# A three-layer field-interaction kernel on one core: bias loads moved to another queue, last weights made earlier, and the end of the last block cut finer

## Chip, core and metric

The kernel runs on one core of one Trainium2 chip, all in fp32. The metric is the device time of one execution in microseconds; the time shown for a kernel is the median of its runs. A profile is one further execution, recorded by the hardware profiler. Its span runs from the first to the last recorded instruction, and the program's own time for that execution is a little longer.

## The reference

```python
B, F, E = 1024, 39, 64          # rows of the input, fields, embedding
HID = [64, 64, 64]

def _cin_layer(Xk, X0, W, b):
    O = W.shape[0]
    Wr = W.reshape(O, Xk.shape[1], X0.shape[1])
    return jnp.einsum('bhe,bfe,ohf->boe', Xk, X0, Wr) + b[None, :, None]

X0 = Xk = sparse_embedding       # (1024, 39, 64)
outs = []
for W, b in ((W0, b0), (W1, b1), (W2, b2)):
    Xk = _cin_layer(Xk, X0, W, b)
    outs.append(Xk.sum(axis=-1))
y = jnp.concatenate(outs, axis=-1) @ fc_w.T + fc_b    # (1024, 1)
```

Each layer multiplies every row of the state with every field of the input, for each embedding position, and mixes the products by a weight. The output needs only sums over the embedding, mixed by `fc_w`.

## The kernel before

**The algebra.** There is no function between the layers, so the last two layers fold into a second linear map of the same pair products. Write P for the products x_a * x_b of two fields (a <= b, with a row of ones as a fortieth field), for one batch row and one embedding position. Then X1 = W0 P, and a second set of 64 rows Z = W' P comes from W1, W2 and `fc_w`. The output of a batch row is the sum over the embedding of (X1 + b0) * (Z + fc0), over 64 rows, plus the fields weighted by 39 numbers made of W2, fc2 and b1, plus one constant made of b1, b2 and fc_b. `wfin` holds the final weights: 64 ones, and below them the 39 weights of the fields. `kfin` is the constant. Both are made on the chip by `last_weights`, which multiplies b1 (present twice, in 128 rows, as `b1s`) with a prepared table `v2`.

**Tiling.** The batch is cut into 32 blocks of 32 batch rows, so 2048 columns (batch row x position). The 819 pair products of a block are packed in six chunks of 128 rows (`PAIRS`), and a small chunk of 32 pair rows for two blocks at once. A chunk's product `p` (128x2048) is one VectorE multiply of two gathered tiles of `rt`. The gathers (`roll`, `roll_small`, L172) are indirect DMAs issued from GpSimd (POOL). They read tables `xd` in DRAM, three of them, each for two blocks; `load` (L166) fills a table from the input and `fill_ones` (L362) writes its row of ones.

**Steps.** `steps` lists (block, chunk): for each pair of blocks n, n+1 the six chunks of n, the small chunk (c = 6, done by `join`, L576 and L587, on 32x64 tiles of the array for both blocks), then the six chunks of n+1. A step's `multiply` (L556) adds its product into four banks `po[n][m]`, one for each quarter m of 512 columns. An fp32 matmul call is two weight loads and two matmuls in the trace, so that a step is 8 matmuls of 512 columns. The order of work is written out by hand: the code emits, step by step, PE's `multiply` of a step and VectorE's `product` four steps ahead (`AHEAD`), with four product buffers. When the chunks of a block are done, `finish` makes z = Z + fc0 on ScalarE (L604), g = (X1 + b0) * z on VectorE (L606) and sums g over the embedding into `sums` (L617). `fields` (L599) has put the block's 39 fields below g, so that the same reduction sums them.

**Start.** A prologue builds index lists and the weights of the chunks: `weight_rows` adds the two orders of a pair, `spread` copies the small chunk's rows, and `weight_turn` transposes a chunk's weights on PE into a bank `tr` (four to a bank, kept in `turned`) and copies them to `wa`. The small vectors are loaded from GpSimd after the gathers of block 1: b0 twice, then b1, b2 and fc_b. GpSimd's queue goes on with `fill_ones(2)` and, in the main loop, with the gathers of the next blocks. SP's queue carries `fill_ones(1)` and the loads of blocks 2 and 3 at the end of step 0, and most later loads. At step 11 (`at == NPAIR + 5`) `spread_b1` doubles b1 with a matmul by `twice`, and at step 12 `last_weights` makes `wfin` and `kfin`, in a bank of its own.

**End.** The last `TAIL` = 2 steps go by quarters: for each quarter m both chunks are multiplied and then `finish_quarter` takes that quarter through z, g and the sum, while PE does the next quarter. Then the final product of `wfin` with `sums` comes in three parts: 512 and 504 columns of the output, and the last 8, which need the last quarter. The first two are copied out with `kfin` by ScalarE (L755), the last by VectorE (L757); ACT's queue stores the first 1016 numbers, SP's queue the last 8.

Of the kernel before, what the change touches and what calls it, by code (L numbers as in the profile page):

```python
# [72 lines left out]
NPAIR = len(PAIRS)  # L73
SQUARE = 32
NCHUNK = NPAIR + 2
MM = 512
SUB = 1024
BLK = 2048
# [4 lines left out]
BB = BLK // E  # L83
SB = SUB // E
NBLK = B // BB
NTAB = 3

U_STEPS = ((10, -29), (20, -8), (23, -2), (25, -36), (28, 32))
V_STEPS = ((0, -3), (20, 6), (25, 33), (28, -35), (31, -39))
# [56 lines left out]
def cin_kernel(ctx: ExitStack, tc: tile.TileContext, x, w0t, b0, w1, b1, w2, b2, fc_w, fc_b, out):  # L146
    nc = tc.nc
# [3 lines left out]
    const = ctx.enter_context(tc.tile_pool(name="const", bufs=1))  # L151
# [39 lines left out]
    bias = const.tile([H, 2], F32, name="bias")  # L191
# [3 lines left out]
    fcb = const.tile([1, 1], F32, name="fcb")  # L195
    wfin = const.tile([H + F, 1], F32, name="wfin")
    kfin = const.tile([1, 1], F32, name="kfin")
# [25 lines left out]
    with prep as prep:  # L223
# [20 lines left out]
        nc.vector.memset(fc2, 0.0)  # L244
        nc.vector.memset(v2, 0.0)
        nc.vector.memset(warm, 0.0)
        nc.sync.dma_start(fcrow, fc_w)
        def load_half(k):
            nc.scalar.dma_start(
# [111 lines left out]
        def fill_ones(k, engine, src):  # L361
            engine.dma_start(xd[k][F::FT].rearrange("r (p c) -> p r c", c=128), src)  # L362
# [33 lines left out]
        for k in range(2):  # L396
            for u in range(2):
# [5 lines left out]
                    start=True,  # L403
                    stop=True,
# [22 lines left out]
        column = blocks.rearrange("h k (f j) -> h (k f) j", j=32)[:, :, 0]  # L427
# [27 lines left out]
        for k, n in enumerate((8, 5)):  # L455
            for t in range(2):
                m = (n + 1 - t) // 2
# [9 lines left out]
        nc.vector.tensor_scalar(lists[:, 2 * NT :], both_of, 2.0, seat, ALU.mult, ALU.add)  # L467
        roll_small(0)
        roll(1)
        for h in (0, H):  # L470
            nc.gpsimd.dma_start(b0s[h : h + H], b0.rearrange("(h o) -> h o", o=1))
        for k, t in enumerate((b1, b2)):
            nc.gpsimd.dma_start(bias[:, k : k + 1], t.rearrange("(h o) -> h o", o=1))
        nc.gpsimd.dma_start(fcb, fc_b.rearrange("(p o) -> p o", o=1))
        fill_ones(2, nc.gpsimd, ones)
        w1v = w1s.rearrange("o (h f) -> o h f", f=F)
        groups = [(k, min(NA * k, F - NA)) for k in range(4)]
        for k, a in groups:
# [4 lines left out]
                start=True,  # L483
                stop=True,
# [46 lines left out]
    turned = []  # L531

    def weight_turn(c):
        place = len(turned) % 4 * 128
        if not place:
            tr = bank("tr")
        else:
            tr = turned[-1]
        turned.append(tr)
        nc.tensor.transpose(tr[:, place : place + 128], pairs[:, c], unit)  # L540
        nc.scalar.copy(wa[:, c, 0 : 2 * H], tr[:, place : place + 2 * H])  # L541
        nc.scalar.copy(wa[:, c, 2 * H :], tr[:, place : place + H])

    work = ctx.enter_context(tc.tile_pool(name="work", bufs=2))
    sums = const.tile([H + F, B], F32, name="sums")
    po, g = {}, {}
# [2 lines left out]
        if n not in po:  # L549
            po[n] = [bank("po") for _ in range(BLK // MM)]  # L550

    def multiply(n, c, p, quarters=range(BLK // MM)):
        open_block(n)
        for m in quarters:
            side = m % 2 * H
            nc.tensor.matmul(  # L556
                po[n][m],
                wa[:, c, side : side + 2 * H],
                p[:, bass.ts(m, MM)],
                start=n % 2 == 0 and c == 0,  # L560
                stop=n % 2 == 1 and c == NPAIR - 1,
            )

    def join(n, p):
# [37 lines left out]
    def finish_bank(n, m, z):  # L602
        one, other = slice(m % 2 * H, m % 2 * H + H), slice((m + 1) % 2 * H, (m + 1) % 2 * H + H)
        nc.scalar.activation(z[one], po[n][m][other], AF.Identity, bias=fc0s[other])  # L604
        at = bass.ts(m % 2, MM)
        return lambda: nc.vector.scalar_tensor_tensor(  # L606
            g[n][m // 2][0:H, at], po[n][m][one], b0s[one], z[one], ALU.add, ALU.mult
        )

    def finish(n):  # L610
# [10 lines left out]
                    ALU.add,  # L621
                )

    def finish_quarter(n, m):
        z = work.tile([128, MM], F32, name="z", tag="z")
        finish_bank(n, m, z)()
        b_at = n * BB + m * MM // E
        nc.vector.tensor_reduce(
            sums[:, b_at : b_at + MM // E],
            g[n][m // 2][:, bass.ts(m % 2, MM)].rearrange("p (b e) -> p b e", e=E),  # L630
            AX.X,
            ALU.add,
        )

    def spread_b1(pk):
        nc.tensor.matmul(
            pk[:, 2:3],
            twice[0:H].rearrange("p h s -> p (h s)"),
            bias[:, 0:1],
            start=True,  # L640
            stop=True,
        )
        nc.scalar.copy(b1s, pk[:, 2:3])

    def last_weights(pk):

        for low, at, n in ((1, 0, 32), (0, 32, F - 32)):
            nc.tensor.matmul(
                pk[at : at + n, 0:1], v2v[:, low, 0, 0:n], b1s, start=True, stop=True
            )  # L650
        fc1 = v2v[:, 0, 0, F - 32 : FT - 32]
        nc.tensor.matmul(pk[0:1, 1:2], b1s, fc1, start=True, stop=False)
        nc.tensor.matmul(
            pk[0:1, 1:2], bias[:, 1:2], columns[0:H, 2:3], start=False, stop=True
        )
        nc.vector.memset(wfin[0:H], 1.0)
        nc.scalar.copy(wfin[H : H + F], pk[0:F, 0:1])
        nc.scalar.activation(kfin, pk[0:1, 1:2], AF.Identity, bias=fcb, scale=float(E))

    AHEAD = 4  # L660
    TAIL = 2
    steps = []
    for n in range(0, NBLK, 2):
        steps += [(n, c) for c in range(NPAIR + 1)] + [(n + 1, c) for c in range(NPAIR)]
# [3 lines left out]
    p = {}  # L668
# [18 lines left out]
    n, c = steps[3]  # L687
# [61 lines left out]
    outv = out.rearrange("b o -> o b")  # L749
    done = B - MM // E  # L750
    for lo, hi in ((0, MM), (MM, done), (done, B)):
        py = bank("py")[0:1, 0 : hi - lo]
        nc.tensor.matmul(py, wfin, sums[:, lo:hi], start=True, stop=True)
        if hi < B:
            nc.scalar.activation(y[:, lo:hi], py, AF.Identity, bias=kfin)  # L755
        else:
            nc.vector.tensor_scalar(y[:, lo:hi], py, kfin, None, ALU.add)  # L757
    nc.scalar.dma_start(outv[:, 0:done], y[:, 0:done])
    nc.sync.dma_start(outv[:, done:B], y[:, done:B])


# [40 lines left out]
```

## Time and profile before

| what | value |
|---|---|
| time of the kernel, median of 3 runs | 735.9 us (734.88 to 737.36) |
| the profiled execution | 734.91 us |
| its span | 733.1 us |
| granted TensorE clock | 1.0 |
| ScalarE, GpSimd busy | 167.7 us, 402.0 us |
| gathers r L172 (156, on POOL) | 1932 ns mean |
| b0 columns L471 (2 issues on POOL) | at 39.14, 8.4 us to landing |
| b1 and b2 columns L473 (2 issues on POOL) | at 40.25, 7.9 us to landing |
| loads of blocks 2 and 3 (2 issues on SP, L166) | at 24.12, 1.78 us of issuing |
| first gather of block 2 (POOL) | at 46.09, after 2.49 us idle |
| store of the last 8 outputs (SP, L759) | issued at 731.01 |

PE is TensorE's matmuls, PEld its weight loads, DVE is VectorE, ACT is ScalarE, POOL is GpSimd and SP is SyncE. A q behind a name is that engine's queue of DMA issues. L556 is line 556 of the kernel. All times are microseconds from the span's start unless marked ns. In a row of a timeline, the bracket at the end tells how long the engine was idle before, and which instruction's end released it. This releaser is inferred: a wait for several things is put down to the one that came last in the records.

### The profile page before, as it was taken

Reading aid. Unit: us, or ns where it says so; the run is one execution under the profiler, and the core shown is the slowest. Engines: PE = TensorE matmul, PEld = TensorE weight load, DVE = VectorE, ACT = ScalarE, POOL = GpSimd, SP = SyncE. Lnnn points to the kernel's source line nnn. Section 1 sums busy time; section 2 is a strip of 40 time slices with the busy share of each in tenths; the row PEclk is TensorE's granted clock in tenths of the full one; section 3 lists DMA queues with packets and bytes.
Section 4 is the critical chain, followed back from the end, with each engine's and each line's share of the span. In section 5 each row is a group of like instructions: output and inputs, shape, how many; then the busy total and the mean of one; then the engine's idle time right before and its main releaser. Section 6 shows DMA issues by size and latency. Waiting matters only on the chain.

```text
span 733.1 us, 6351 instructions
## 1 busy us (share of the span) xinstructions
PE 728.0 (99%) x2377; PEld 314.9 (43%) x2377; DVE 638.4 (87%) x520; ACT 167.7 (23%) x241; POOL 402.0 (55%) x254
## 2 busy tenths in 40 slices
PE   9999999999999999999999999999999999999998
PEld 4444444444444444444444444444444444444443
DVE  6979799988889888898988889888898888889885
ACT  3322121222212222121221212221122221212222
POOL 7769998537555455654547545455654447535300
PEclk9999999999999999999999999999999999999999
DMA  8887898979575796757778675896767876566700
GB/s 291 305 318 294 300 355 304 383 293 331 232 270 231 287 355 252 281 226 262 314 287 304 245 275 226 305 353 219 279 246 275 313 286 264 214 253 245 287 0 1
DMA packets 65979, 197.23 MB, mean 269 GB/s; under 512 B 40109, under 2 KB 40174, under 8 KB 45980
## 3 DMA queue, kind: packets, MB, share of 16 engines
q0 software_dynamic: 28784, 185.56, 65.3%
q1 hardware_dynamic: 35464, 9.28, 5.5%
q10 hardware_dynamic: 1700, 1.99, 0.9%
q8 instruction: 18, 0.29, 0.1%
q14 instruction: 13, 0.11, 0.0%
HBM read 196.76 MB, written 10.60 MB: 283 GB/s over the span
## 4 chain that ended last, share of the span: by engine, by line
PE 93%; DVE 2%; POOL 2%; DMA 1%; issue 1%; ACT 0%; DVEq 0%
PE po L556 86%; PE po L576 4%; PE po L587 2%; DMA b0s<-in_b 1%; POOL r L172 1%; DVE p L217 1%; PE idle L276 1%; POOL u L172 1%; DVE g L606 1%; POOL v L172 0%; DVE pairs L523 0%; PE pv L399 0%; PE pt L479 0%; PE pw L411 0%; DVE sums L617 0%
## 5 line engine op out<-in xcount | busy, mean ns | idle before, releaser
L556 PE MATMUL po<-p,wa 128*128 128x512 f32 x1536 | 665.7, 594 | 0.7 <-DVE p L217 0.6
L217 DVE TENSOR_TENSOR p<-r 128x2048 f32<-128x2048 f32 (+2 forms) x197 | 433.8, 2235 | 74.5 <-PE po L556 69.9
L556 PEld LDWEIGHTS po<-p,wa 128*128 128x128 f32 x1536 | 289.7, 190 | 371.3 <-issue 350.5
L172 POOL DMA_INDIRECT r<-xd,lists x156 | 301.4, 1932 | 263.9 <-issue 259.5
L604 ACT ACTIVATE z<-po,columns 64x512 f32<-64x512 f32 x128 | 87.4, 683 | 371.9 <-PE po L587 219.1
L606 DVE SCALAR_TENSOR_TENSOR g<-po,b0s,z 64x512 f32<-64x512 f32 x128 | 95.9, 749 | 9.3 <-ACT z L604 5.3
L599 ACT COPY g<-r 39x1024 f32<-39x1024 f32 x64 | 66.7, 1043 | 157.2 <-DVE sums L617 125.2
L617 DVE TENSOR_REDUCE sums<-g 103x16 f32<-103x1024 f32 x62 | 75.6, 1220 | 2.1
L172 POOL DMA_INDIRECT u<-xd,lists x16 | 41.8, 2612 | 8.3 <-issue 4.6
L172 POOL DMA_INDIRECT v<-xd,lists x16 | 41.1, 2569 | 4.9 <-issue 4.9
L576 PE MATMUL po<-p,wa 32*64 32x512 f32 x512 | 31.6, 600 | 0.0
L219 DVE TENSOR_TENSOR p<-u,v 128x1024 f32<-128x1024 f32 x16 | 19.5, 1219 | 0.0
L576 PEld LDWEIGHTS po<-p,wa 32*64 32x64 f32 x512 | 9.4, 131 | 20.2 <-issue 20.2
L587 PE MATMUL po<-u,wa 32*64 32x512 f32 x256 | 17.0, 587 | 0.0
L172 POOL DMA_INDIRECT r<-xh,lists x8 | 7.6, 956 | 3.8 <-issue 2.1
L587 PEld LDWEIGHTS po<-u,wa 32*64 32x64 f32 x256 | 5.7, 132 | 8.0 <-issue 8.0
L276 PE MATMUL idle<-const-float32-1.0 128*128 128x512 f32 (+2 forms) x12 | 7.7, 732 | 0.8 <-PEq L789 0.8
L523 DVE TENSOR_TENSOR pairs<-both 128x2 f32<-128x2 f32 (+27 forms) x59 | 6.1, 171 | 0.1
L541 ACT COPY wa<-tr 128x128 f32<-128x128 f32 x8 | 2.1, 266 | 14.8 <-PE tr L540 14.8
L276 PEld LDWEIGHTS idle<-const-float32-1.0 128*128 128x128 f32 x12 | 2.5, 253 | 1.9 <-issue 1.7
L166 POOL DMA_DIRECT2D xd<-in_x x3 | 3.2, 1060 | 0.0
L488 DVE STREAM_TRANSPOSE flat<-pt 128x320 f32<-128x320 f32 x2 | 1.0, 516 | 2.2 <-PE pt L479 2.2
(96 smaller groups left out, 57.3 us busy)
## 6 DMA issues: line engine op xcount, KB each, us to landing
xd<-in_x SPq DMA_DIRECT2D x28, 312.0 KB
r<-xd,lists POOLq DMA_INDIRECT x156, 9.0
xd<-in_x POOLq DMA_DIRECT2D x3, 312.0 KB, 7.7
w2s<-in_w ACTq DMA_DIRECT2D x1, 624.0 KB
w1s<-in_w ACTq DMA_DIRECT2D x1, 624.0 KB
w0s<-in_w0t ACTq DMA_DIRECT2D x1, 380.2 KB
xh<-in_x ACTq DMA_DIRECT2D x2, 156.0 KB
xd<-xh SPq DMA_DIRECT2D x2, 156.0 KB
```

The costliest lines, as they stand in the source:

```text
L172: nc.gpsimd.indirect_dma_start(dst, None, table, bass.IndirectOffsetOnAxis(ap=lists[:, k : k + 1], axis=0))
L217: nc.vector.tensor_tensor(p[:, cols], r[:, i, cols], r[:, k, cols], ALU.mult)
L219: nc.vector.tensor_tensor(p[:, 0:SUB], ut[n // 2 % 2], vt[n // 2 % 2], ALU.mult)
L276: nc.tensor.matmul(idle[:, 0:cols], nc.const_aps.tensor(1.0, (128, 128), F32), nc.const_aps.tensor(1.0, (128, cols), F32), start=True, sto ...
L523: nc.vector.tensor_tensor(out, diagonal(a, b, sa, sb), diagonal(b, a, sb, sa), ALU.add)
L556: nc.tensor.matmul(po[n][m], wa[:, c, side : side + 2 * H], p[:, bass.ts(m, MM)], start=n % 2 == 0 and c == 0, stop=n % 2 == 1 and c == NP ...
L576: nc.tensor.matmul(dst[half * H : half * H + H], wa[rows, NPAIR, at : at + H], p[rows, bass.ts(side, MM)], start=t >= 2, stop=t < 2 and ha ...
L587: nc.tensor.matmul(dst[half : half + H], wa[rows, NPAIR + 1, H : 2 * H], ut[n // 2 % 2][rows, bass.ts(side, MM)], start=False, stop=t < 2,)
L599: nc.scalar.copy(gt[H : H + F], rt[n % 2][0:F, 0, bass.ts(m, SUB)])
L604: nc.scalar.activation(z[one], po[n][m][other], AF.Identity, bias=fc0s[other])
L606: return lambda: nc.vector.scalar_tensor_tensor(g[n][m // 2][0:H, at], po[n][m][one], b0s[one], z[one], ALU.add, ALU.mult)
L617: nc.vector.tensor_reduce(sums[:, b_at : b_at + SB], g[n][m // 2].rearrange("p (b e) -> p b e", e=E), AX.X, ALU.add,)
```

## The change

Five edits come together.

1. The small vectors are no longer loaded from GpSimd after the gathers of block 1. A new function `load_biases` loads them from SP, between `fill_ones(1)` and the loads of blocks 2 and 3, at the end of step 0. b1 is read twice by the transfer itself, each element to two neighbouring rows of `b1s`; b2 has a tile of its own; fc_b goes to 96 rows. `spread_b1` is gone.
2. `last_weights` runs at step 5 (`at == NPAIR - 1`), behind the last `weight_turn`, and uses the first `tr` bank. It makes the constant in 96 rows. The memset of the ones in `wfin` goes to the head of the prologue.
3. `TAIL` is 3: the last three chunks go by quarters.
4. The last quarter is done in two pieces of 256 columns, each taken through the three chunks, z, g and the sum (`finish_piece`).
5. The output is cut in four quarters of 256. The first three are made by three matmuls, each to its own 32 columns of the array (`wfin` repeated 32 times), into 96 rows of one bank; one ScalarE instruction adds the constant, and ACT's queue stores three rows. The last quarter comes in 252 and 4 columns, and SP's queue stores its 256 numbers at once.

```diff
+NY = 3
+YB = B // 4
...
+        nc.vector.memset(wfin[0:H], 1.0)
         nc.sync.dma_start(fcrow, fc_w)
...
-        for h in (0, H):
-            nc.gpsimd.dma_start(b0s[h : h + H], b0.rearrange("(h o) -> h o", o=1))
-        for k, t in enumerate((b1, b2)):
-            nc.gpsimd.dma_start(bias[:, k : k + 1], t.rearrange("(h o) -> h o", o=1))
-        nc.gpsimd.dma_start(fcb, fc_b.rearrange("(p o) -> p o", o=1))
         fill_ones(2, nc.gpsimd, ones)
...
-    def multiply(n, c, p, quarters=range(BLK // MM)):
+    def multiply(n, c, p, quarters=range(BLK // MM), piece=slice(0, MM)):
         open_block(n)
         for m in quarters:
             side = m % 2 * H
             nc.tensor.matmul(
-                po[n][m],
+                po[n][m][:, piece],
                 wa[:, c, side : side + 2 * H],
-                p[:, bass.ts(m, MM)],
+                p[:, m * MM + piece.start : m * MM + piece.stop],
...
-    def spread_b1(pk):
...
+    def load_biases():
+        def column(t):
+            return t.rearrange("(h o) -> h o", o=1)
+
+        for h in (0, H):
+            nc.sync.dma_start(b0s[h : h + H], column(b0))
+        nc.sync.dma_start(b1s, column(b1).to_broadcast([H, 2]))
+        nc.sync.dma_start(b2s, column(b2))
+        nc.sync.dma_start(fcb, column(fc_b).to_broadcast([NY * 32, 1]))
...
-        nc.tensor.matmul(pk[0:1, 1:2], b1s, fc1, start=True, stop=False)
+        total = pk[0 : NY * 32, 1:2]
+        nc.tensor.matmul(total, b1s.to_broadcast([128, NY * 32]), fc1, start=True, stop=False)
         nc.tensor.matmul(
-            pk[0:1, 1:2], bias[:, 1:2], columns[0:H, 2:3], start=False, stop=True
-        )
-        nc.vector.memset(wfin[0:H], 1.0)
+            total, b2s.to_broadcast([H, NY * 32]), columns[0:H, 2:3], start=False, stop=True
+        )
         nc.scalar.copy(wfin[H : H + F], pk[0:F, 0:1])
-        nc.scalar.activation(kfin, pk[0:1, 1:2], AF.Identity, bias=fcb, scale=float(E))
+        nc.scalar.activation(kfin, total, AF.Identity, bias=fcb, scale=float(E))
...
-    TAIL = 2
+    TAIL = 3
...
             if at == NPAIR - 1:
                 weight_turn(NPAIR + 1)
+                last_weights(turned[0])
...
             fill_ones(1, nc.sync, ones1)
+            load_biases()
             for k in (2, 3):
                 load(k)
...
-        if at == NPAIR + 5:
-            pk = bank("pk")
-            spread_b1(pk)
-        if at == NPAIR + 6:
-            last_weights(pk)
...
-    for m in range(BLK // MM):
+    ends = [(m, slice(0, MM)) for m in range(BLK // MM - 1)]
+    ends += [(BLK // MM - 1, slice(k, k + MM // 2)) for k in (0, MM // 2)]
+    for m, piece in ends:
         for n, c in steps[-TAIL:]:
-            multiply(n, c, p[n, c], (m,))
-        finish_quarter(NBLK - 1, m)
-
-    y = const.tile([1, B], F32, name="y")
...
+            multiply(n, c, p[n, c], (m,), piece)
+        finish_piece(NBLK - 1, m, piece)
+
+    y = const.tile([NY * 32, YB], F32, name="y")
+    yl = const.tile([1, YB], F32, name="yl")
+    outv = out.rearrange("(t b) o -> t (b o)", b=YB)
+    done = YB - MM // 2 // E
+    py = bank("py")
+    for t in range(NY):
+        nc.tensor.matmul(
+            py[32 * t : 32 * t + 32, 0:YB],
+            wfin.to_broadcast([H + F, 32]),
+            sums[:, t * YB : t * YB + YB],
+            start=True,
+            stop=True,
+        )
+    nc.scalar.activation(y, py[0 : NY * 32, 0:YB], AF.Identity, bias=kfin)
+    nc.scalar.dma_start(outv[0:NY], y[0 : NY * 32 : 32])
+    for lo, hi in ((0, done), (done, YB)):
         py = bank("py")[0:1, 0 : hi - lo]
-        nc.tensor.matmul(py, wfin, sums[:, lo:hi], start=True, stop=True)
-        if hi < B:
-            nc.scalar.activation(y[:, lo:hi], py, AF.Identity, bias=kfin)
+        nc.tensor.matmul(
+            py, wfin, sums[:, NY * YB + lo : NY * YB + hi], start=True, stop=True
+        )
+        if hi < YB:
+            nc.scalar.activation(yl[:, lo:hi], py, AF.Identity, bias=kfin[0:1])
         else:
-            nc.vector.tensor_scalar(y[:, lo:hi], py, kfin, None, ALU.add)
-    nc.scalar.dma_start(outv[:, 0:done], y[:, 0:done])
-    nc.sync.dma_start(outv[:, done:B], y[:, done:B])
+            nc.vector.tensor_scalar(yl[:, lo:hi], py, kfin[0:1], None, ALU.add)
+    nc.sync.dma_start(outv[NY : NY + 1], yl)
```

`finish_bank` and `finish_piece` are `finish_bank` and `finish_quarter` of before with the columns of the piece in place of those of the quarter.

More of the change, by code (lines that the diff above doesn't have):

```diff
@@ L190, in cin_kernel @@
     twice = const.tile([128, H, 2], F32, name="twice")
-    bias = const.tile([H, 2], F32, name="bias")
+    b2s = const.tile([H, 1], F32, name="b2s")
     b1s = const.tile([128, 1], F32, name="b1s")
@@ L194, in cin_kernel @@
     fc0s = columns[:, 1:2]
-    fcb = const.tile([1, 1], F32, name="fcb")
+    fcb = const.tile([NY * 32, 1], F32, name="fcb")
     wfin = const.tile([H + F, 1], F32, name="wfin")
-    kfin = const.tile([1, 1], F32, name="kfin")
+    kfin = const.tile([NY * 32, 1], F32, name="kfin")
     lists = const.tile([128, 2 * NT + 2], I32, name="lists")
@@ L556, in multiply @@
             nc.tensor.matmul(
-                po[n][m],
+                po[n][m][:, piece],
                 wa[:, c, side : side + 2 * H],
-                p[:, bass.ts(m, MM)],
+                p[:, m * MM + piece.start : m * MM + piece.stop],
                 start=n % 2 == 0 and c == 0,
                 stop=n % 2 == 1 and c == NPAIR - 1,
+                skip_group_check=piece.start > 0,
             )
@@ L600, in fields, with finish_bank @@
             g[n].append(gt)
-    def finish_bank(n, m, z):
+    def finish_bank(n, m, z, piece=slice(0, MM)):
         one, other = slice(m % 2 * H, m % 2 * H + H), slice((m + 1) % 2 * H, (m + 1) % 2 * H + H)
-        nc.scalar.activation(z[one], po[n][m][other], AF.Identity, bias=fc0s[other])
-        at = bass.ts(m % 2, MM)
+        part = po[n][m][:, piece]
+        nc.scalar.activation(z[one, piece], part[other], AF.Identity, bias=fc0s[other])
+        at = slice(m % 2 * MM + piece.start, m % 2 * MM + piece.stop)
         return lambda: nc.vector.scalar_tensor_tensor(
-            g[n][m // 2][0:H, at], po[n][m][one], b0s[one], z[one], ALU.add, ALU.mult
+            g[n][m // 2][0:H, at], part[one], b0s[one], z[one, piece], ALU.add, ALU.mult
         )
@@ L622, in finish, with finish_piece @@
                 )
-    def finish_quarter(n, m):
+    def finish_piece(n, m, piece):
         z = work.tile([128, MM], F32, name="z", tag="z")
-        finish_bank(n, m, z)()
-        b_at = n * BB + m * MM // E
+        finish_bank(n, m, z, piece)()
+        b_at = n * BB + (m * MM + piece.start) // E
+        at = m % 2 * MM
         nc.vector.tensor_reduce(
-            sums[:, b_at : b_at + MM // E],
-            g[n][m // 2][:, bass.ts(m % 2, MM)].rearrange("p (b e) -> p b e", e=E),
+            sums[:, b_at : b_at + (piece.stop - piece.start) // E],
+            g[n][m // 2][:, at + piece.start : at + piece.stop].rearrange(
+                "p (b e) -> p b e", e=E
+            ),
             AX.X,
@@ L633, in finish_quarter @@
         )
-    def spread_b1(pk):
[L636 to L641, printed above, removed]
-        )
-        nc.scalar.copy(b1s, pk[:, 2:3])
+    def load_biases():
[6 more added lines that the diff above has]
+        nc.sync.dma_start(fcb, column(fc_b).to_broadcast([NY * 32, 1]))
     def last_weights(pk):
@@ L740, in cin_kernel @@
                     load(n + 4, nc.gpsimd)
-    for m in range(BLK // MM):
+    ends = [(m, slice(0, MM)) for m in range(BLK // MM - 1)]
+    ends += [(BLK // MM - 1, slice(k, k + MM // 2)) for k in (0, MM // 2)]
+    for m, piece in ends:
         for n, c in steps[-TAIL:]:
-            multiply(n, c, p[n, c], (m,))
-        finish_quarter(NBLK - 1, m)
-    y = const.tile([1, B], F32, name="y")
-    outv = out.rearrange("b o -> o b")
-    done = B - MM // E
-    for lo, hi in ((0, MM), (MM, done), (done, B)):
-        py = bank("py")[0:1, 0 : hi - lo]
-        nc.tensor.matmul(py, wfin, sums[:, lo:hi], start=True, stop=True)
-        if hi < B:
-            nc.scalar.activation(y[:, lo:hi], py, AF.Identity, bias=kfin)
-        else:
-            nc.vector.tensor_scalar(y[:, lo:hi], py, kfin, None, ALU.add)
-    nc.scalar.dma_start(outv[:, 0:done], y[:, 0:done])
-    nc.sync.dma_start(outv[:, done:B], y[:, done:B])
+            multiply(n, c, p[n, c], (m,), piece)
[16 more added lines that the diff above has]
+    for lo, hi in ((0, done), (done, YB)):
+        py = bank("py")[0:1, 0 : hi - lo]
+        nc.tensor.matmul(
[3 more added lines that the diff above has]
+            nc.scalar.activation(yl[:, lo:hi], py, AF.Identity, bias=kfin[0:1])
+        else:
+            nc.vector.tensor_scalar(yl[:, lo:hi], py, kfin[0:1], None, ALU.add)
+    nc.sync.dma_start(outv[NY : NY + 1], yl)
 def kernel(
```

## The prediction

> **What bounds the kernel now.** I read the page first, for the engine that is full.
>
> ```profile
> PE 728.0 (99%) x2377; PEld 314.9 (43%) x2377; DVE 638.4 (87%) x520; ACT 167.7 (23%) x241; POOL 402.0 (55%) x254
> ...
> L556 PE MATMUL po<-p,wa 128*128 128x512 f32 x1536 | 665.7, 594 | 0.7 <-DVE p L217 0.6
> ```
>
> TensorE is busy for 728 us of a span of 733.1. Its groups of 96 matmuls of 512 columns take 41.40 us in the chain, 0.431 us each; the edit removes none of these columns. So only three places can pay: a hole in PE's stream, small PE work that stands in the stream, and what lies before and after it. I read these from the chain in order of time (start, length, what).
>
> ```profile
> 57.63 3.70 PE po L556 x8
> 61.33 0.31 PE pk L636 x2
> 61.64 3.63 PE po L556 x8
> 65.27 0.15 PE pk L648 x3
> 65.42 0.05 PE pk L652 x2
> 65.47 0.12 PE pk L653 x2
> ...
> 728.20 0.69 ACT z L604
> ...
> 728.91 0.77 DVE g L606
> ...
> 729.70 0.70 DVE sums L628
> ...
> 730.53 0.21 PE py L753 x2
> ...
> 730.77 0.21 DVE y L757
> ```
>
> The chain is PE without a break from 57.63 to 728.17, with 0.31 + 0.32 = 0.63 us of pk matmuls in it. After 728.17 come five short steps and the store. Before 57.63 it runs over VectorE. PE's own timeline shows the hole there (bracket: idle before, and what ended it).
>
> ```profile
> 37.43 0.33 PE L540 MATMUL tr<-unit,pairs 128*128 128x128 f32 x1 [0.47 <-ACT wa L542]
> ...
> 43.02 14.00 PE L556 MATMUL po<-p,wa 128*128 128x512 f32 x32
> 57.63 3.70 PE L556 MATMUL po<-p,wa 128*128 128x512 f32 x8 [0.61 <-DVE p L217]
> ```
>
> PE idles 0.61 us until the product of step (1,4) is there. VectorE had worked without a gap worth 0.5 us since 40.39, when it began step (1,0) after 4.55 us of waiting. The view names PE, but the buffer it needs was free by about 33; the second gather of `roll(1)` was issued at 32.31 to 35.00, and the next two products wait on gathers by name, so I read that wait as its landing. The chain also names the b0 transfer, landing at 47.97; its reader at 49.78 followed straight on a product, so it cost nothing.
>
> **What the skill says.** The page "DMA: Bandwidth & Descriptors", section "Queues, rings and completion order", says that each of the 16 engines goes round the queues in turn, a packet at a time. Transfers from SP then don't stand behind GpSimd's gathers, only beside them. The trace fits: the b0 columns, issued from GpSimd behind five gathers, took 8.4 us to land. SP's two loads of 24.12 are 2 x 1248 pieces of 256 B, 156 per engine if spread over 16; the gather that reads them starts at 46.09, so a piece took at most (46.09 - 24.12) / 156 = 0.14 us. I go by this estimate below. "TensorE: Matmul & The Clock Gate", section "Part 3: Packing small matmuls", gives 2.38 times for three column tiles. Here 32 matmuls of 512 columns on tiles of 32x64 take 1.90 us instead of 32 x 0.431 = 13.8, so tiles do run together; I go by the trace.
>
> **The change, part by part.**
>
> *Bias preparation.* `spread_b1` goes: 0.31 us of PE at 61.33 and a 0.16 us ACT copy. `last_weights` moves from 65.27 to just behind the transpose of 37.43: its eight matmuls take 0.32 us, a little more with weights 96 columns wide, say 0.37. There it lies before the hole: 0.61 - 0.37 leaves 0.24, and PE still waits for the same product at 57.63. So 0.63 us go and nothing comes back: **-0.63**. Without the cover the move alone would be worth nothing and the sum -0.26.
>
> *The new wait.* In its new place PE waits for b1 (and b2). Behind it on PE stand the rest of step (0,5) and the join of 40.26; ACT's copies into `wfin` and `kfin` also wait for fc_b, and behind those stands the first z, due at 43.09, 4 us later. The join may also need the bank that these copies read, by 40.6. The transfers leave SP after `fill_ones` (23.73, 0.34 us each), at about 24.1 to 25.8. They have 64 + 64 + 128 + 64 + 96 = 416 pieces, 26 per engine: 26 x 0.14 = 3.6 us at the loads' pace, plus about 2 us (SP's last store, 731.01 to the end at 733.1): landed by 30 to 32. Even with the 8.4 us of the loaded queue they are there at 34.2, and PE asks at 37.7. I take no wait; the far bound is the loads' own 22 us, so 46 and 8 us of stall.
>
> *What SP and POOL get.* POOL loses five issues (1.16 + 1.10 + 0.63 = 2.9 us from 39.14); behind them `fill_ones` waited for a gather until 43.04 and `roll(2)` until 46.09, so nothing is won. On SP the loads of blocks 2 and 3 leave 5 x 0.34 = 1.7 us later. `roll(2)` then starts up to 1.7 us later, perhaps less, as the DMA engines get through the same bytes; 3.6 if the pieces also queue. Its first product starts at 59.87, against issue by 50.72: hidden. The closer place is block 3: VectorE waits for its gathers at 80.76, 85.19 and 88.59, and the product of (3,4) ends at 100.9, while PE needs it at 89.15 + 4 x 3.45 = 102.95. That margin of 2.0 becomes 1.4 when PE is 0.63 earlier. Value taken 0; bounds -0.2 (the gathers of block 1 meet less traffic, and the 0.24 left of the hole closes) and +2.2 (3.6 - 1.4).
>
> *Memset of wfin* (0.06 us of VectorE at 66.33) goes to the start, ahead of a 0.36 us idle at 2.48: 0. Without that cover, 0.06.
>
> *The last quarter in two pieces.* Columns are the same, but 12 matmuls have 256 instead of 512 in 6. No row has 256 at full pace; four of 320 (pv L479, 1.18 us) take 0.295 each against 320/512 x 0.431 = 0.269. I take these 0.026 for each: 12 x 0.026 = **+0.3**; bounds 0 and 0.6.
>
> *Three chunks by quarters.* The last product, (31,5), is now asked for by the 29th of the 48 last matmuls, not the 33rd: 707.29 + 28 x 0.43 = 719.3, its weights at 718.99. VectorE has it at 719.16 (two products from 714.68, 4.48 us). So PE slips: **+0.1**, between 0 and 0.3.
>
> *After the last matmul.* Call its end T. Before: z 0.69, g 0.77, sum 0.70, ending at T+2.23. Slopes: ACT 0.833 ns a column (y of 512 columns 679 ns, one column of kfin 253), VectorE 1.06 for g (749 against 214 for the 8 columns of L757), 1.04 for the sum (1220 of 1024 against 686 of 512). So 256 columns take 0.47, 0.48 and 0.42. The quarter before ends at T-2.6, its z, g and sum by T-0.4; the first half ends at T-1.3, its z by T-0.8, g and sum by T+0.55. The second half: z to T+0.5, g to T+1.06, sum to T+1.51. **-0.72**. Both sums fit because three chunks stretch a quarter to 2.6 us; at two it would be 1.7 and VectorE would be late.
>
> *The fields' sum.* Three column tiles of 256 columns need only old sums: 0.43 us together, 1.3 one by one, where before 512 and 504 columns stood (1.86 us, hidden). ACT then has y (96 rows x 256, 0.47), its DMA issue (0.27) and the 252-column y (0.46): T+0.6 to about T+2.0, or T+2.6 if the tiles don't overlap. The last four columns follow as before (0.13 + 0.21 + 0.03 + 0.21) and end at T+2.1. So they meet, and the store leaves at T+2.1 instead of T+2.84: 0, at worst +0.55. The stored 1 KB instead of 32 B I take as 0.
>
> Sum: -0.63 + 0.3 + 0.1 - 0.72 = -0.95, so -1.0. The span becomes 732.1, and the profiled execution 734.91 - 1.0 = 733.9. That execution lay 1.0 under the median of 735.9, so the median goes to **734.9**, 0.13% less. A measurement of this kernel can hardly tell less than 0.3% (2.2 us) from no change: its three runs span 2.5 us.
>
> **The rivals.**
>
> *More gain.* The half pieces cost nothing (-0.3), PE doesn't slip (-0.1), and fewer loads beside the gathers of block 1 close the hole by 0.2: -1.6, 734.3. For it: DMA engines were near full in 34 to 46. Against: 0.295 for 320 columns, and that the total of bytes doesn't fall. Chance 0.12.
>
> *The gathers take the gain back.* The loads of blocks 2 and 3 land 2.4 us late, `roll(2)` and then `roll(3)` pass it on, and the product of (3,4) is 2.4 - 1.4 = 1.0 late: 735.9. For it: POOL stood 12.44 us in one gather at 54.76, so it has no time to give; against: DMA was at a 0.39 share in 24 to 26, when the small pieces run, and much can be caught up between 66 and 68 (0.09). Chance 0.2.
>
> *Slower: PE stands for b1 in `last_weights`.* It decides from a landing at 37.9 on (37.7 and the 0.24 of the hole). At 41 PE loses 41 - 37.9 = 3.1 us, and with the -1.0 the time is 738.0. For it: transfers of 4-byte pieces beside gathers of 8 KB rows, in engines with a share of 0.92 from 26 on, and a load that took up to 22 us. Against: 26 pieces per engine are a sixth of that load's, and they come first. Chance 0.1.
>
> **How the numbers follow.** The forecast has 0.55; 0.03 stays for what I don't see. The range holds the forecast and both bounds of the known terms, with some 0.8 us for the median of a few runs: 733.4 to 737.2; the slower rival is left out. Faster by over 0.3% means under 733.7: the lower edge of the forecast (0.1) and a good part of the first rival, 0.17. Slower means over 738.1: half of the last rival, the edge of the second and the unforeseen, 0.11. The rest, 0.72, lies within.
>
> **What would show it.** Right: PE idle near 57 is 0.2 to 0.3 us instead of 0.61, no pk matmul after it, `last_weights` near 37.7 with no wait; the span's end about 4.2 us behind the last main matmul instead of 4.9; PE without a hole at 103. Wrong: PE idle ahead of the first pk matmul, a new hole named after a product between 60 and 110, over 0.5 us of idle near 719, or ACT's last y behind VectorE's at the end.

## The result and the profile after

| | before | after |
|---|---|---|
| median | 735.29 us (733.78 to 737.36, 22 runs) | 737.03 us (736.05 to 739.6, 22 runs) |
| ratio, with its 95% interval | | 1.0025 [1.0017, 1.0032] |
| the profiled execution | 734.91 us | 736.05 us |
| its span | 733.1 us | 734.2 us |

The changed kernel is slower by 0.25%, 1.3 to 2.4 us. The forecast was 734.9, a gain of 0.95 on the 735.9 of the three runs known then. From the page of the changed kernel, the row of the engines and the group of main matmuls:

```profile
PE 727.2 (99%) x2385; PEld 316.2 (43%) x2385; DVE 639.3 (87%) x522; ACT 167.4 (23%) x241; POOL 385.6 (53%) x249
...
L554 PE MATMUL po<-p,wa 128*128 128x512 f32 x1542 | 665.5, 592 | 2.0 <-DVE g L606 1.5
```

TensorE is busy for 0.8 us less than before. But 2.0 us of idle now stand ahead of its main group, 1.5 of them in one wait ended by a `g` of VectorE. Before, this row had 0.7, ended by products.

The timeline of all engines at the end shows where (start, length, engine and line, tiles; in the bracket the idle before and its releaser):

```profile
726.41 0.47 ACT L604 ACTIVATE z<-po,columns 64x256 f32<-64x256 f32 x1 [0.61 <-PE po L554]
726.60 0.69 DVE L629 TENSOR_REDUCE sums<-g 103x8 f32<-103x512 f32 x1
727.32 0.49 DVE L606 SCALAR_TENSOR_TENSOR g<-po,b0s,z 64x256 f32<-64x256 f32 x1
...
727.87 1.56 PE L554 MATMUL po<-p,wa 128*128 128x256 f32 x6 [1.50 <-DVE g L606]
729.36 0.63 PE L755 MATMUL py<-sums,wfin 103*32 103x256 f32 x6
729.47 0.47 ACT L604 ACTIVATE z<-po,columns 64x256 f32<-64x256 f32 x1 [2.59 <-PE po L554]
...
730.55 0.82 ACTq L763 DMA_DIRECT2D out_y<-y  x1
...
731.42 0.46 ACT L770 ACTIVATE yl<-py,kfin 1x252 f32<-1x252 f32 x1 [0.90 <-PE py L766]
731.91 0.27 SPq L773 DMA_DIRECT2D out_y<-yl  x1
```

TensorE ends the first half of the last quarter, waits while ScalarE makes its z and VectorE its g, and only then begins the second half. The six matmuls after the wait take 1.56 us. Part of the wait is VectorE's order of work: z of the first half is there at 726.88, but VectorE still sums the quarter before (the row at 726.60) and comes to this g at 727.32.

The other end of the stream, in the chain of waits (start, length, what):

```profile
37.95 0.33 PE tr L538
38.28 0.15 PE tr L650 x3
38.43 0.26 PE tr L655 x2
38.69 0.26 PE tr L656 x2
38.94 2.77 PE po L554 x6
41.72 1.90 PE po L575 x32
43.62 0.86 PE po L586 x16
44.48 30.67 PE po L554 x71
```

The small matmuls follow the transpose at once, so there is no wait for b1. The join (L575) starts at 41.72 instead of 40.33, and the idle near 57 is gone: the stream goes on from 44.48 without a break. (Joins begin 0.07 us earlier in a timeline than in a chain, 41.65 here. The chain before doesn't pass through its first join; the timeline has that at 40.26, so I take 40.33, and likewise for other kernels.)

To compare kernels I cut the span at the start of the first join and at that of the last one (block 30). What lies ahead of the first is the **start**, between the two is the **stream**, behind the last is the **end**.

| profiled execution | first join | last join | stream | span | end |
|---|---|---|---|---|---|
| before | 40.33 | 704.60 | 664.27 | 733.1 | 28.5 |
| after | 41.72 | 704.09 | 662.37 | 734.2 | 30.1 |

So the stream became 1.90 us shorter, the end 1.6 us longer, and the start was 1.39 us later.

### The profile page after: what moved, and what is told of

Its sections match the earlier page's. It is cut to its first block, busy times and chain, and to the rows that moved or that the text cites. A ratio compares the mean times of both kernels' runs of the same rounds, so it can differ in the third digit from the quotient of the medians.

```text
span 734.2 us, 6372 instructions
## 1 busy us (share of the span) xinstructions
PE 727.2 (99%) x2385; PEld 316.2 (43%) x2385; DVE 639.3 (87%) x522; ACT 167.4 (23%) x241; POOL 385.6 (53%) x249
## 4 chain that ended last, share of the span: by engine, by line
PE 95%; DVE 1%; DMA 1%; POOL 1%; issue 0%; ACT 0%; ACTq 0%
PE po L554 89%; PE po L575 4%; PE po L586 2%; DMA r<-xh,lists 1%; POOL r L174 1%; DVE p L219 1%; PE idle L279 0%; DVE g L606 0%; POOL xd L168 0%; DVE pairs L521 0%; ACTq L763 0%; ACT z L604 0%; DVE sums L629 0%; PE tr L538 0%; PE py L755 0%
## 5 line engine op out<-in xcount | busy, mean ns | idle before, releaser
L174 POOL DMA_INDIRECT r<-xd,lists x156 | 313.3, 2008 | 281.1 <-issue 265.6
L174 POOL DMA_INDIRECT u<-xd,lists x16 | 29.9, 1866 | 7.6 <-issue 4.3
L575 PE MATMUL po<-p,wa 32*64 32x512 f32 x512 | 31.6, 600 | 0.0
L174 POOL DMA_INDIRECT v<-xd,lists x16 | 27.5, 1718 | 4.9 <-issue 4.9
L575 PEld LDWEIGHTS po<-p,wa 32*64 32x64 f32 x512 | 9.4, 131 | 20.2 <-issue 20.2
L629 DVE TENSOR_REDUCE sums<-g 103x8 f32<-103x512 f32 (+1 forms) x5 | 2.9, 579 | 0.2
```

Of the source, the lines that this page charges most:

```text
L174: nc.gpsimd.indirect_dma_start(dst, None, table, bass.IndirectOffsetOnAxis(ap=lists[:, k : k + 1], axis=0))
L575: nc.tensor.matmul(dst[half * H : half * H + H], wa[rows, NPAIR, at : at + H], p[rows, bass.ts(side, MM)], start=t >= 2, stop=t < 2 and ha ...
```

## The experiments

The theory: both halves lie in one bank of PSUM (the memory into which TensorE writes its results), `po[31][3]`, and the second half's matmuls wait until the first half has been read. Rivals: the pieces of 256 columns are slow as such; the bias loads from SP delay something; or the start does it.

**The last quarter whole again** (all else as changed):

```diff
-    ends = [(m, slice(0, MM)) for m in range(BLK // MM - 1)]
-    ends += [(BLK // MM - 1, slice(k, k + MM // 2)) for k in (0, MM // 2)]
+    ends = [(m, slice(0, MM)) for m in range(BLK // MM)]
...
-    done = YB - MM // 2 // E
+    done = YB - MM // E
```

> The changed kernel with the last quarter whole (four quarters of 512 columns, the output cut in 248 and 8 columns at its end); all else of the change stays. Theory (bank wait): in the changed kernel PE stood 1.50 us before the second half, until g had read the first half out of the same bank; here this idle is gone, no matmul of 256 columns is left in the last block, and z, g and sum of the last quarter take 2.2 us instead of 1.5. Net about 1.1 to 1.5 us less than the changed kernel, so 735.5 to 736.0 where before is 735.3 (ratio to before 0.9995 to 1.001). Rival (the start is what lost): the time stays near 737, ratio 1.002 to 1.003.

Measured: 736.73 us, ratio 1.0018 [1.0003, 1.0032]. The idle before the end is gone, and the end takes 28.7 us. The time didn't follow: it lies outside what the theory expected and nearer to the rival, though with a wide interval. The granted clock, the share of its full clock that TensorE was let have, tells more. In this profiled execution it was 0.58 from 18 to 26 us, where the changed kernel has 1.00, and the first join began at 45.03. Of the 11 runs, 5 have a mean clock of 0.996 or less (median 737.21 us) and 3 of 0.999 or more (734.86 us). Of the 50 runs of the kernel before beside them, 6 are of the first kind (737.10) and 22 of the second (734.99). So the excess goes with the clock; why this kernel met the lower clock more often isn't shown. The idle is tied to the halves; what it costs is left to the next runs.

**Halves multiplied first, finished afterwards:**

```diff
             multiply(n, c, p[n, c], (m,), piece)
-        finish_piece(NBLK - 1, m, piece)
+        if not (piece.start == 0 and piece.stop < MM):
+            if piece.start:
+                finish_piece(NBLK - 1, m, slice(0, MM // 2))
+            finish_piece(NBLK - 1, m, piece)
```

> The changed kernel, but both halves of the last quarter are multiplied before either is taken through z, g and sum. Theory (bank wait): the half pieces are still there, but PE has no reason to wait between them: its idle of 1.50 us goes, and 2.3 us of z, g, sum, g, sum follow the last matmul instead of 1.5. Net 0.6 us less than the changed kernel (ratio to before 1.001 to 1.002). If PE still idles about 1.5 us between the halves, the wait is not for the reading of the first half and the theory falls.

Measured: 735.87 us, 1.0008 [0.9999, 1.0018]; no idle between the halves, end 29.2 us. The matmuls are the same twelve of 256 columns, so it isn't their size that costs; it is the reading between them.

**Edits 3 and 4 alone**, put on the kernel before (`TAIL` 3, halves, `finish_piece`; output as before with the cut at 508):

```diff
-    TAIL = 2
+    TAIL = 3
...
-    for m in range(BLK // MM):
+    ends = [(m, slice(0, MM)) for m in range(BLK // MM - 1)]
+    ends += [(BLK // MM - 1, slice(k, k + MM // 2)) for k in (0, MM // 2)]
+    for m, piece in ends:
...
-    done = B - MM // E
+    done = B - MM // 2 // E
```

> The kernel before, with three chunks by quarters and the last quarter in two pieces, and nothing else (its own output in 512, 508 and 4 columns). Theory (bank wait): PE idles 1.5 us between the halves and the short matmuls cost 0.3, against 0.7 less after the last matmul: 0.8 to 1.3 us slower than before, ratio 1.001 to 1.002. Rival (the start is what lost): 0.4 us faster than before, as the prediction had it for the end, ratio about 0.9995, no idle.

Measured: 736.80 us, 1.0024 [1.0016, 1.0033]. The view of waits of this kernel (engine, what waited, for what; total, times, longest):

```profile
PE po L556 <- DVE g L608: 1.5, 1, 1.5
```

These two edits alone make a loss as large as that of the whole change. It is more than I expected. The end here is 30.1 us, as in the changed kernel, though the output isn't cut in quarters: its two long output products, hidden before, come after the late last half and take 1.86 us at 730.46.

**Edits 1 and 2 alone** (the end of the kernel before; the diff is against the changed kernel):

```diff
-    TAIL = 3
+    TAIL = 2
...
+    for m in range(BLK // MM):
...
-            multiply(n, c, p[n, c], (m,), piece)
-        finish_piece(NBLK - 1, m, piece)
+            multiply(n, c, p[n, c], (m,))
+        finish_piece(NBLK - 1, m, slice(0, MM))
...
+    for lo, hi in ((0, MM), (MM, done), (done, B)):
```

> The kernel before, with the bias loads from SP, b1 twice by its transfer, the last weights at step 5 and the memset early; the end as before (two chunks by quarters, whole last quarter, output on one row). Theory: these edits win what was forecast, 0.5 to 1.0 us faster than before, ratio 0.9986 to 0.9994, with no hole in PE near 57 and no small matmuls after it. Rival (the start is what lost): 1 to 2 us slower, ratio 1.0015 to 1.003, with PE late at the first join.

Measured: 735.48 us, 1.0002 [0.9994, 1.0011]. A miss: the stream is 662.37 us, as in the changed kernel, but the gain isn't in the time. The first join of the profiled execution starts at 42.95.

**The second half in a bank of its own:**

```diff
-            multiply(n, c, p[n, c], (m,), piece)
+            if piece.start:
+                if c == steps[-TAIL][1]:
+                    po[n][m] = bank("po")
+                ...
+                    po[n][m][:, piece],
+                ...
+                    start=c == steps[-TAIL][1],
+            else:
+                multiply(n, c, p[n, c], (m,), piece)
```

> The changed kernel, but the second half of the last quarter is added up in a bank of its own. It leaves out what the shared bank held for these four batch rows (the first three chunks and the small chunk of the last block); the instructions after and before are the same in number and size. Theory (the two halves wait for each other because they share a bank): PE's idle of 1.50 us between the halves goes, though z, g and sum of the first half run beside the second half's matmuls, and the time after the last matmul stays as short as in the changed kernel (about 1.5 us to the last sum). About 1.5 us less than the changed kernel, ratio to before 1.0002 to 1.0010. Rival (PE waits for VectorE as such, or for the order of the code): the idle stays 1.5 us and the ratio 1.0025.

Measured: 734.96 us against 734.95 for the kernel before, 1.0000 [0.9990, 1.0009]; end 28.3 us. Its timeline, with the same columns as above:

```profile
725.71 0.74 DVE L606 SCALAR_TENSOR_TENSOR g<-po,b0s,z 64x512 f32<-64x512 f32 x1 [1.04 <-ACT z L604]
...
726.09 1.46 PE L750 MATMUL po<-p,wa 128*128 128x256 f32 x6
726.29 0.47 ACT L604 ACTIVATE z<-po,columns 64x256 f32<-64x256 f32 x1 [0.61 <-PE po L554]
...
727.21 0.49 DVE L606 SCALAR_TENSOR_TENSOR g<-po,b0s,z 64x256 f32<-64x256 f32 x1
...
727.48 0.63 PE L767 MATMUL py<-sums,wfin 103*32 103x256 f32 x6
```

Now the second half is multiplied while z and g of the first are made; no idle stands in the bracket of L750. In this kernel's chain the six matmuls take 1.29 us from 726.25, 0.215 each, which is half of 0.431: pieces of 256 run at full pace. The theory stands: with the second half in a bank of its own, z and g of the first no longer hold it up. The wait itself is one for a semaphore, so it is part of the program as built; what the chip would do without it, and whether the bank or the tile it belongs to is what the program keeps apart, these runs can't tell, as this edit changes both. The end shows one thing more: even without the wait it is only 0.2 us shorter than before.

**The loads on SP alone** (b1 twice by the transfer, no doubling matmul; the last weights at step 12 and the end as before; the diff is against the kernel before):

```diff
-        for h in (0, H):
-            nc.gpsimd.dma_start(b0s[h : h + H], b0.rearrange("(h o) -> h o", o=1))
...
+            load_biases()
...
-            spread_b1(pk)
```

> The kernel before with the bias loads on SP as in the change (b1 twice by its transfer, so the doubling matmul is gone); the last weights stay at step 12 and the end as before. Theory (the hole near 57 goes because the gathers of block 1 meet no loads of blocks 2 and 3, and from then on PE alone sets the pace from its first matmuls on): no hole in PE between 45 and 110, VectorE's first g 2 to 3 us earlier than 49.8, and 0.3 to 0.9 us faster than before, ratio 0.9988 to 0.9996, if PE's first join is where it was (40.3 to 40.9). Against the kernel with the weights at step 5 as well it saves 0.3 to 0.5 us. Rival (these loads harm the start): first join after 41.5 and ratio 1.0002 or more.

Measured: 735.22 us, 1.0000 [0.9991, 1.0009]. The idle near 57 was gone, as expected, and the stream was 662.89 us. The time stayed, which is a miss. The first join was at 41.85, late as the rival had it, but without the loss that the rival had with it.

**The memset of `wfin` back in `last_weights`**, on top of edits 1 and 2, as this is the one edit executed before 24 us:

```diff
-        nc.vector.memset(wfin[0:H], 1.0)
         nc.sync.dma_start(fcrow, fc_w)
...
+        nc.vector.memset(wfin[0:H], 1.0)
         nc.scalar.copy(wfin[H : H + F], pk[0:F, 0:1])
```

> The kernel with the bias edits alone, but the memset of the ones in wfin is back in last_weights, so that the prologue is instruction for instruction that of before. Rival (the added instruction at the head of the prologue makes the start late): first join at 40.9 to 41.3 instead of 42.95, and 0.5 to 1.0 us faster than with the memset early, ratio 0.9990 to 0.9996. Theory (the start varies from execution to execution, whatever the memset): ratio 0.9996 to 1.0008 as with the memset early, and a first join anywhere from 41.2 on.

Measured: 735.36 us, 1.0007 [0.9999, 1.0016], first join at 41.94. The memset isn't what makes the start late.

**The last weights after the last main matmul**: whole quarter, `last_weights` in front of the last `finish_piece`, its copy into `wfin` on VectorE, the store of y on SP. This takes their small matmuls out of the start and out of the stream:

```diff
-        nc.scalar.copy(wfin[H : H + F], pk[0:F, 0:1])
+        nc.vector.tensor_copy(wfin[H : H + F], pk[0:F, 0:1])
...
-                last_weights(turned[0])
...
+        total = last_weights(bank("pk")) if m == BLK // MM - 1 else None
         finish_piece(NBLK - 1, m, piece)
+    last_constant(total)
...
-    nc.scalar.dma_start(outv[0:NY], y[0 : NY * 32 : 32])
+    nc.sync.dma_start(outv[0:NY], y[0 : NY * 32 : 32])
```

> The changed kernel with the last quarter whole, the small matmuls of last_weights behind the last main matmul (where PE waits for z, g and sum anyway), the copy into wfin on VectorE while ScalarE makes the last z, and the store of three rows issued from SP. Theory (small matmuls cost their full time wherever PE sets the pace): nothing but main matmuls between the first and the last, 0.8 us less than with the weights at step 5 and a whole last quarter at equal starts, and no wait for ACT's store at the end: ratio to before 0.9985 to 1.0002. If it is no faster than before (ratio above 1.0005), the start takes back what the stream wins.

Measured: 735.03 us, 1.0000 [0.9992, 1.0008]; end 29.0 us. No form of the change that I ran was faster than the kernel before; this one and `loads_only` equal it.

**Was the start late because of the change?** Eight profiles of kernels with the loads on SP had their first join at 41.6 or later; those with the loads on GpSimd, two of them, at 40.33 and 41.02. So I profiled the kernel before twice more, and the last one once.

> The kernel before, unchanged, profiled once more. Theory: the start varies from one execution to the next whatever the kernel, and in the kernel before a late start is covered by the hole near 57 (0.61 us with the first join at 40.26). Then the first join starts anywhere from 40.3 to 42.5, and where it is later than 40.9 the idle of TensorE near 57 is gone. Rival: only kernels that load the biases from SP start late. Then the first join starts from 40.2 to 41.0, and ScalarE has no idle of over 1.5 us between 12 and 20.

> A second look at the kernel before, with the same two readings: theory, first join from 40.3 to 42.5 and the idle near 57 smaller by as much as the join is later; rival, first join from 40.2 to 41.0 and no long idle of ScalarE before 20.

> late_weights once more. Theory: the start varies by execution; first join from 40.3 to 42.5, not always the 41.69 seen. Rival: it is late in every execution of a kernel with the loads on SP; first join at 41.5 or later again, with an idle of ScalarE of 1.6 us or more between 12 and 20.

Measured: the unchanged kernel began its first join at 44.71 and 44.01 (738.38 and 737.71 us), with no idle near 57 in either; `late_look` began it at 41.28. The theory was right in kind, though the start varies more than its range allowed; the rival falls. Whether the change makes a late start more frequent, so few profiles can't tell. The chain of the first of these looks at the kernel before:

```profile
41.80 0.33 PE tr L540
42.13 2.58 PE po L556 x6
44.71 1.90 PE po L576 x32
46.61 0.86 PE po L587 x16
47.47 17.36 PE po L556 x40
64.83 0.31 PE pk L636 x2
65.14 3.63 PE po L556 x8
...
```

This is the profile that the prediction lacked. TensorE never stands between the first join and the last, so the stream is what its work takes: 663.40 us to the last join at 708.11, and 663.40 in the other look too. In the profile that the prediction read, the stream was 664.27: it held 0.87 us more, 0.61 of it the idle near 57, which an early start had bought. The start of this look was late in two steps. The first is in ScalarE's first copy into `wa`:

```profile
19.17 0.27 ACT L541 COPY wa<-tr 128x128 f32<-128x128 f32 x1 [3.77 <-remote]
```

It came 2.40 us later than in the first profile (16.77), after an idle put down to "remote", which names no instruction of this core. The second step is in the first six main matmuls, here in the first profile and then in this look:

```profile
17.09 1.13 PE L556 MATMUL po<-p,wa 128*128 128x512 f32 x2
...
18.43 1.95 PE L556 MATMUL po<-p,wa 128*128 128x512 f32 x4
```

```profile
19.49 2.07 PE L556 MATMUL po<-p,wa 128*128 128x512 f32 x2 [2.65 <-ACT wa L541]
...
21.57 3.62 PE L556 MATMUL po<-p,wa 128*128 128x512 f32 x4
```

They took 5.69 us instead of 3.08, and the granted clock from 18 to 26 us was 0.57 in this look instead of 1.00. At the transpose behind the next sixteen matmuls the look is 4.38 us late (32.14 against 27.76), so some 2.0 us of it came with the lower clock. In the second look ScalarE's copy is 3.05 us late, and the clock was 0.79. Six of the 13 profiles have such a lower clock there, with the change and without it. The opposite case is `late_look`, in TensorE's timeline:

```profile
44.27 14.00 PE L554 MATMUL po<-p,wa 128*128 128x512 f32 x32 [0.23 <-DVE p L219]
59.21 1.13 PE L554 MATMUL po<-p,wa 128*128 128x512 f32 x2 [0.94 <-DVE p L219]
```

With an early start a hole of 0.94 us is there again in spite of the loads on SP, behind a gather that landed at 46.8. So the two ways into the stream, TensorE's own start and block 1's gathers with their products, are both of varying length, and the later one decides. The median before, 735.3 us, would go with a first join near 41.6 (735.3, less 1.8 outside the span, 28.5 of end and 663.4 of stream), an estimate by which the start decides in the middle execution too.

## Why the prediction was wrong

The changed kernel against the kernel before, in executions in which the start decides: the stream loses the small matmuls, 662.37 - 663.40 = -1.03; the last weights come into the start, +0.86 (from the transpose to the join 3.77 us, 37.95 to 41.72, against 2.91, 41.80 to 44.71); and the end changes by what its row shows. The same sum for the other kernels, each beside what was measured (ratio less one, times 735.3):

| kernel | stream | weights at start | end | sum | measured, us |
|---|---|---|---|---|---|
| after | -1.03 | +0.86 | +1.6 | +1.4 | +1.8 [1.3, 2.4] |
| whole_quarter | -1.03 | +0.86 | +0.2 | 0.0 | +1.3 [0.2, 2.4] |
| halves_after | -1.03 | +0.86 | +0.7 | +0.5 | +0.6 [-0.1, 1.3] |
| halves_only | 0 | 0 | +1.6 | +1.6 | +1.8 [1.2, 2.4] |
| bias_only | -1.03 | +0.86 | +0.2 | 0.0 | +0.1 [-0.4, 0.8] |
| own_bank | -1.03 | +0.86 | -0.2 | -0.4 | 0.0 [-0.7, 0.7] |
| loads_only | -0.51 | 0 | +0.2 | -0.3 | 0.0 [-0.7, 0.7] |
| memset_back | -1.03 | +0.86 | +0.2 | 0.0 | +0.5 [-0.1, 1.2] |
| late_weights | -1.03 | 0 | +0.5 | -0.5 | 0.0 [-0.6, 0.6] |

All but whole_quarter, whose clock differed, have their sum within the interval. At a mean clock of 0.999 or more the changed kernel's 11 runs have a median of 736.42 us and the 8 of halves_only 736.39, both 1.4 above the 734.99 of the kernel before. Most of the intervals hold zero too: what the times show is the +1.6 of the end, while the smaller terms rest on the profiles. Every measured value is at or above its sum, by some 0.4 us on average; what that is, and how much of it belongs to the clock or to the loads on SP, these runs can't tell.

**The failing step: "After the last matmul".** It ended the first half at T-1.3 and let TensorE go on with the second half while the first one's z and g were made, -0.72. That second half waited for this very g. The prediction looked for readers of the second half's results, not for readers of the bank it writes to. The Trainium skill has the rule, on its page "PSUM — Partial Sum Buffer", section "PSUM bank collisions raise a hardware error": accesses by different engines are to be kept apart by bank and by group of 32 partitions, not by address. What stands beside it here is the 1.50 us ahead of 727.87, and its absence in own_bank: in this program, as built, the second half isn't written until the first has been read. From the last join to T the changed kernel takes 25.34 us (704.09 to 729.43) instead of 23.57, so +1.77: 1.50 of wait, and 0.27 by which the second half is slower after it (1.56 against 1.29). From T to the span's end it is 4.77 instead of 4.93, a gain of 0.16 instead of 0.72.

**After T**, the path through z, g and the last sum was right: 730.91, T+1.48, against T+1.51. The one beside it was not: ACT's issue of the store of three rows took 0.82 us instead of the 0.27 assumed, so the 252-column copy behind it ended at 731.88 and the store left at T+2.48, not T+2.1. In own_bank, without the wait, it still leaves at T+2.47 (730.02), so the gain of 0.72 had a second hole in it.

**Bias preparation.** The removal was worth more than -0.63: the main matmuls beside the small ones also run slower (40 in 17.36 and 8 in 3.63 us, where 0.431 each makes 17.24 and 3.45), and the whole is -1.03. But putting the last weights in the start costs 0.86, not 0.37, and the hole that was to cover it isn't there in most profiles. As a sum it is -0.17 where the start decides, not -0.63. The text gave the value "without the cover" too, and took the cover from a single execution, an early one at full clock.

**Half pieces**: 0, not +0.3 (own_bank, 0.215 each). **Slip by three chunks**: 0, not +0.1: 42 matmuls in 18.24 us from 706.85, 0.434 each, the pace of the 48 in 20.81 before. **Column tiles**: six matmuls of 256 columns in 0.60 us, half of 6 x 0.215, so they do run together.

**The rivals.** The wait for b1 didn't come about: TensorE asks at 38.28 and goes on. SP's queue in the changed kernel:

```profile
23.99 1.20 SPq L643 DMA_DIRECT2D b0s<-in_b  x2
25.23 0.60 SPq L644 DMA_DIRECT2D b1s<-in_b  x1
...
26.51 0.58 SPq L646 DMA_DIRECT2D fcb<-in_fc_b  x1
27.14 19.73 SPq L168 DMA_DIRECT2D xd<-in_x  x4
```

A load of one column costs 0.60 us of SP's time, not 0.34, so the loads of blocks 2 and 3 leave at 27.14 instead of 24.12, 3.0 us later and not 1.7. Still the gathers didn't take the gain back: block 2's first gather starts at 46.47 instead of 46.09, and TensorE has no hole at 103. "More gain" had the hole closed and the pieces free of cost, both of which the profile shows, but stood on the same end. That the measured 737.03 lies in the stated range of 733.4 to 737.2 is luck: its upper part was meant for late gathers, dearer pieces and the scatter of a median, and no term of it was a wait between the halves.

## What to carry to other kernels

Before a last piece of work is cut so that its reading overlaps its writing, look at which PSUM bank each piece lies in: with both pieces in one bank the cut makes a chain of what ran side by side, here for 1.6 us. A hole in one profile covers a cost only if it is there in other executions too, so profile the start more than once before spending it, and read the granted clock there. Small matmuls in a full TensorE stream cost more than their own time, here 1.03 us for 0.63.

## What the runs showed that was not expected

- The start of one and the same kernel varies by 4.4 us between profiles (first join 40.33, 44.71, 44.01). Two parts are seen: ScalarE's first copy into `wa`, at 16.77, 19.17 and 19.82, and a granted clock of 1.00, 0.57 and 0.79 from 18 to 26 us. What ScalarE waits for there stays open; the records name "remote" in seven of the 13 profiles and a matmul in six. The clock is open too. In the six profiles with a lower clock TensorE had stood for 1.84 us or more ahead of its first main matmul, but own_bank stood for 1.85 and kept 1.00.
- Issue on a queue depends on the shape: 0.27 us for one row, 0.60 for a column of 64 or 128 single numbers, 0.82 on ACT's queue and 0.76 on SP's for three rows of 1 KB.
- With the loads of blocks 2 and 3 sent 3 us later, the first g, of block 0, came at 47.17 instead of 49.78. Other profiles of such kernels agree (46.4 to 48.0 in six more), but one has 51.35, and one with a late start 49.48, so this isn't sure to hold.
